# A four-layer convolution and attention kernel: another scheduling model, and a higher priority for the attention's work on VectorE and ScalarE

## The chip, the core and the metric

One core of a Trainium2 chip runs the whole kernel. The metric is the device time of one execution in microseconds (us); the figure that counts is the median of several runs. TensorE (PE in the profile; PEld is its loading of weights) multiplies matrices, VectorE (DVE) and ScalarE (ACT) work elementwise, GpSimd (POOL) does a few small powers, and SyncE (SP) issues all the DMAs. Every engine works through its own queue of instructions in order; semaphores tie the queues together.

## The reference

Four images of 256 channels and 64 x 64 points pass through four layers, each with a group normalisation before it and a residual sum behind it, all in float32.

```
x = x + L0(gn(x))   # 3x3 convolution, group norm, ReLU -> xs;  full attention over the
                    # 4096 points:  f = theta^T phi;  y = softmax(f) g;  1x1 conv, norm;  0.1*. + xs
x = x + L1(gn(x))   # linear attention: q, k, v of 4 heads x 32; context = k v^T; 1x1 conv, rms norms
x = x + L2(gn(x))   # generated kernels: depthwise 3x3 and pointwise 256x256, both from pooled x
x = x + L3(gn(x))   # mixture of four 256x256 experts, weights from pooled x
```

The attention of layer 0 has no shift by a row's maximum in the exponent here; sums are checked at the end and a general version would run if they left a safe range (it doesn't run with these inputs).

## The kernel before

The kernel is written in a tile language: the program text says what is computed in which tile, and a scheduler that plays the program through a model of the machine fixes the order of every engine's queue and the buffers. Among the instructions that are ready at a time of that model, the scheduler takes the one with the lowest priority number; the number counts up with the program text, so what stands earlier in the text goes first.

The work on an image falls into these parts.

- `convolve(b)`: group normalisation of the image in `xp`, a 3x3 convolution in a transformed (Winograd) form. `down` and `across` (DVE) make the inputs `v`, PE multiplies them with filters `u` that a DMA fetches from DRAM (`ps_conv`, line 325), DVE and ACT add the results up in `big`. Then a normalisation (`smoothed`), whose result xs stays in `big` and goes to DRAM (`xs_d`).
- `project()`: PE makes `theta`, `phi` and `g` from `big` (`ps_tp`, `ps_g`, lines 365 and 370) into the tile `tpg`.
- `attend(b)`: the full attention, in 8 query blocks of 512 points. A block has 16 steps `m`; a step makes two tiles `pf` = phi^T theta on PE (line 387), two exponentials on ACT into one tile `pr` (line 388), two products `py` += g pr on PE (line 397), and one sum `tot` += pr on DVE (recorded at the helper's line 62). The logits of step m+1 are written ahead of the products of step m. At the end of a block come `inv` (DVE, line 404), the column sum `pss` (PE, line 407), a reciprocal (DVE, line 408), a check value `junk` (ACT, line 410) and `yt` = py * inv (DVE), which a DMA writes to `y_d`.
- `tail(b)`: `nonlocal_out` (reads `y_d`, `ps_wy`, the residual of layer 0), `linear_attention` (layer 1), `generated` (layer 2: `dw`, eight multiply-adds a tile on DVE at the helper's line 65, then `ps_pw` on PE) and `mixed` (layer 3: `ps_ex`).

`pr` has three buffers, `pf` two banks of PSUM, `py` and `pss` share two banks, `tot` and `inv` have one buffer each. `junk` and `yt` share five buffers (`k2`) with small tiles of the layers.

`tpg` and `big` exist once. So `project()` for the next image waits until the attention on the present one is done and the next image's convolution too, and the next tail follows the projection. The loop over images is written so that the attention of image b, which comes last in the text of iteration b, stands beside the tail of image b-1 and the convolution of image b+1:

```
    for b in range(B):
        if b > 0:
            tail(b - 1)
        if b + 1 < B:
            load_x(b + 1)
            convolve(b + 1)
        attend(b)
        if b + 1 < B:
            project()
    tail(B - 1)
```

Of the kernel before, what the change touches and what calls it, by code (L numbers as in the profile page):

```python
# [8 lines left out]
F32 = mybir.dt.float32  # L9
AF = mybir.ActivationFunctionType  # L10
ALU = mybir.AluOpType
AX = mybir.AxisListType

P = 128
# [3 lines left out]
CH = 1024  # L18
# [21 lines left out]
def conv_preact_fast(ctx: ExitStack, tc: tile.TileContext, guard, x, wc, wtpg, ww, wqkv, wout, w1cat, wd2,  # L40
# [3 lines left out]
    nc = tc.nc  # L44
# [3 lines left out]
    wk = ctx.enter_context(tc.tile_pool(name="work", bufs=1))  # L48
    sp = ctx.enter_context(tc.tile_pool(name="small", bufs=2))
    pp = ctx.enter_context(tc.tile_pool(name="ps", bufs=1, space=bass.MemoryType.PSUM))  # L50
# [4 lines left out]
    def k2(name):  # L55
        return wk.tile([P, 512], F32, tag="k2", name=name, bufs=5)
# [4 lines left out]
    def tt(o, a, b, op):  # L61
        nc.vector.tensor_tensor(o, a, b, op)  # L62
# [18 lines left out]
    def load_x(b):  # L81
        for h in range(NH):
            for q in range(2):
                rows = bass.ts(q, HW // 2)
                nc.sync.dma_start(out=xin[:, h, rows, :],
                                  in_=x[b, bass.ts(h, P), bass.ts(q, N // 2)].rearrange("p (y x) -> p y x", x=HW))
# [32 lines left out]
    ones = cp.tile([P, P], F32, name="ones")  # L119
# [238 lines left out]
    def project():  # L358

        for c in range(N // 512):  # L360
            cols = bass.ts(c, 512)
            for k in (1, 0):
                ps = bank("ps_tp")
                for h in range(NH):
                    nc.tensor.matmul(ps, wtpg_s[:, h, k, :], big[:, h, cols], start=(h == 0), stop=(h == NH - 1))  # L365
                nc.scalar.activation(tpg[:, k, cols], ps, AF.Identity, bias=btp_s[:, k:k + 1])
            ps = bank("ps_g").rearrange("p (j o) -> p j o", o=P)
            for j in range(4):
                for h in range(NH):
                    nc.tensor.matmul(ps[:, j, :], big[:, h, bass.ts(4 * c + j, P)], wtpg_s[:, h, 2, :],  # L370
                                     start=(h == 0), stop=(h == NH - 1))
            tt(g[:, cols].rearrange("p (j o) -> p j o", o=P), ps, bg_s.unsqueeze(1).to_broadcast([P, 4, P]), ALU.add)

    def attend(b):
        NM = N // CH * 4
        for q in range(NQ):
            cols = bass.ts(q, 512)
            at = b * NQ + q
            py = pp.tile([P, 512], F32, tag="acc", name="py", bufs=2)
            tot = wk.tile([P, CH], F32, tag="tot", name="tot")  # L380
            probs = {}

            def logits(m):
                pr = wk.tile([P, CH], F32, tag="pr", name="pr", bufs=3)
                for s in range(2):
                    pf = pp.tile([P, 512], F32, tag="pf", name="pf", bufs=2)
                    nc.tensor.matmul(pf, phi[:, bass.ts(2 * m + s, P)], theta[:, cols], start=True, stop=True)  # L387
                    nc.scalar.activation(pr[:, bass.ts(s, 512)], pf, AF.Exp)  # L388
                probs[m] = pr

            logits(0)
            for m in range(NM):
                if m + 1 < NM:
                    logits(m + 1)
                pr = probs[m]
                for s in range(2):
                    nc.tensor.matmul(py, g[:, bass.ts(2 * m + s, P)], pr[:, bass.ts(s, 512)],  # L397
                                     start=(m == 0 and s == 0), stop=(m == NM - 1 and s == 1))
                if m == 1:
                    tt(tot, probs[0], pr, ALU.add)  # L400
                elif m > 1:
                    tt(tot, tot, pr, ALU.add)
            inv = wk.tile([P, 512], F32, tag="inv", name="inv")
            nc.vector.scalar_tensor_tensor(inv, tot[:, 0:512], 1.0, tot[:, 512:CH], ALU.mult, ALU.add,
                                           accum_out=guard[:, 0, at:at + 1])
            pss = pp.tile([P, 512], F32, tag="acc", name="pss", bufs=2)
            nc.tensor.matmul(pss, ones, inv, start=True, stop=True)  # L407
            nc.vector.reciprocal(inv, pss)  # L408
            junk = k2("junk")
            nc.scalar.activation(junk, inv, AF.Copy, accum_out=guard[:, 1, at:at + 1])  # L410
            yt = k2("yt")
            tt(yt, py, inv, ALU.mult)
            nc.sync.dma_start(out=y_d[b, :, cols], in_=yt)


# [237 lines left out]
    def tail(b):  # L653
        mixed(b, generated(b, linear_attention(b, nonlocal_out(b))))
# [3 lines left out]
    convolve(0)  # L658
    project()
    for b in range(B):  # L660
        if b > 0:
            tail(b - 1)
        if b + 1 < B:
            load_x(b + 1)
            convolve(b + 1)
        attend(b)
        if b + 1 < B:
            project()
    tail(B - 1)
# [502 lines left out]
@with_exitstack  # L1172
def conv_preact_kernel(ctx: ExitStack, tc: tile.TileContext, *args):
    nc = tc.nc
    B = args[0].shape[0]
    gp = ctx.enter_context(tc.tile_pool(name="guard", bufs=1))
    guard = gp.tile([P, 2, B * NQ + 1], F32, name="guard")
    conv_preact_fast(tc, guard, *args)


    fit = gp.tile([P, 2, B * NQ + 1], F32, name="fit")
    for side in range(2):
        nc.vector.tensor_scalar(fit[:, side, :], guard[:, side, :], GUARD_MAX[side], None, ALU.is_le)
    low = gp.tile([P, 1], F32, name="low")
    nc.vector.tensor_reduce(low, fit.rearrange("p s k -> p (s k)"), AX.X, ALU.min)
    every = gp.tile([P, P], F32, name="every")
    nc.gpsimd.memset(every, 1.0)
    good = gp.tile([P, 1], mybir.dt.int32, name="good")
    with tc.tile_pool(name="guard_ps", bufs=1, space=bass.MemoryType.PSUM) as gps:
        count = gps.tile([P, 1], F32, name="count")  # L1190
        nc.tensor.matmul(count, every, low, start=True, stop=True)
        nc.vector.tensor_scalar(good, count, P - 0.5, None, ALU.is_ge)
    in_range = nc.values_load(good[0:1, 0:1], min_val=0, max_val=1)
    with tc.If(in_range < 1):
        conv_preact_general(tc, *args)
# [58 lines left out]
```

## Time and profile before

| | |
|---|---|
| median of 3 runs | 3769.94 us (3769.51 to 3772.02) |
| the profiled execution | 3772.22 us |
| its span, first to last instruction | 3770.4 us |
| mean granted TensorE clock | 0.912 |
| busy: PE, DVE, ACT, POOL | 3150.8, 2208.6, 1125.4, 88.9 us |
| HBM traffic | 40 GB/s over the span |

The profile shows one execution. Its page gives busy times, then the span in 40 equal slices (a digit is a busy share in tenths), then groups of instructions with the mean duration of one. A view by stretches gives busy times between two moments. In this span the iterations of the loop lie, to a few us, at 225 to 802 (b = 0), 802 to 1709 (b = 1), 1709 to 2608 (b = 2) and 2608 to 3363 (b = 3); the tail of the last image follows to the end. Instructions of the small helpers for elementwise work on DVE are all recorded at lines 62 and 65, so that they are told apart by their tiles. Matmuls in float32 are recorded as two instructions each.

### The profile page before, as it was taken

Reading aid. Unit: us, or ns where it says so; the run is one execution under the profiler, and the core shown is the slowest. Engines: PE = TensorE matmul, PEld = TensorE weight load, DVE = VectorE, ACT = ScalarE, POOL = GpSimd, SP = SyncE. Lnnn points to the kernel's source line nnn. Section 1 sums busy time; section 2 is a strip of 40 time slices with the busy share of each in tenths; the row PEclk is TensorE's granted clock in tenths of the full one; section 3 lists DMA queues with packets and bytes.
Section 4 is the critical chain, followed back from the end, with each engine's and each line's share of the span. In section 5 each row is a group of like instructions: output and inputs, shape, how many; then the busy total and the mean of one; then the engine's idle time right before and its main releaser. Section 6 shows DMA issues by size and latency. Waiting matters only on the chain.

```text
span 3770.4 us, 24367 instructions
## 1 busy us (share of the span) xinstructions
PE 3150.8 (84%) x8322; PEld 1498.2 (40%) x8322; DVE 2208.6 (59%) x2696; ACT 1125.4 (30%) x2111; POOL 88.9 (2%) x133
## 2 busy tenths in 40 slices
PE   4699999989956889998984879999897699967645
PEld 2254444445422334444531334445452244434412
DVE  8869344353697944436479773444567734452476
ACT  2122333335410033333540013333443033323220
POOL 0000000001000000000100000000010000000000
PEclk9899999999977999999996889999998799987667
DMA  5313000020012220001001230000101200020011
GB/s 184 124 35 104 24 6 3 9 73 1 1 52 80 64 90 3 6 20 59 1 26 54 80 117 3 6 9 23 51 1 40 83 6 6 9 67 6 0 31 51
DMA packets 84484, 151.20 MB, mean 40 GB/s; under 512 B 8960, under 2 KB 46592, under 8 KB 82176
## 3 DMA queue, kind: packets, MB, share of 16 engines
q1 hardware_dynamic: 84352, 149.57, 11.6%
q8 instruction: 68, 1.11, 0.1%
q14 instruction: 64, 0.52, 0.0%
HBM read 101.30 MB, written 48.23 MB: 40 GB/s over the span
## 4 chain that ended last, share of the span: by engine, by line
PE 66%; DVE 21%; issue 7%; ACT 3%; POOL 2%; DMA 0%; SPq 0%; POOLq 0%; ACTq 0%; DVEq 0%
PE pf L387 20%; PE py L397 20%; PE ps_conv L325 9%; DVE dw L65 8%; PE ps_ex L647 3%; PE ps_tp L365 3%; DVE big L65 3%; PE ps_qkv L471 2%; PE ps_h L545 2%; PE ps_g L370 1%; PE ps_wy L425 1%; DVE z L62 1%; ACT junk L515 1%; DVE st L598 1%; PE ps_o L510 1%
## 5 line engine op out<-in xcount | busy, mean ns | idle before, releaser
L388 ACT ACTIVATE pr<-pf 128x512 f32<-128x512 f32 x1024 | 604.6, 596 | 1437.8 <-PE pf L387 1105.9
L62 DVE TENSOR_TENSOR tot<-tot,pr 128x1024 f32<-128x1024 f32 x448 | 547.9, 1223 | 826.1 <-ACT pr L388 825.7
L387 PE MATMUL pf<-tpg 128*128 128x512 f32 x2048 | 989.3, 605 | 22.7 <-ACT pr L388 22.7
L397 PE MATMUL py<-pr,tpg 128*128 128x512 f32 x2048 | 976.9, 600 | 11.1 <-DVE ev L62 7.7
L387 PEld LDWEIGHTS pf<-tpg 128*128 128x128 f32 x2048 | 385.7, 193 | 508.8 <-issue 419.1
L397 PEld LDWEIGHTS py<-pr,tpg 128*128 128x128 f32 x2048 | 390.6, 193 | 489.4 <-issue 471.7
L325 PE MATMUL ps_conv<-v,u 128*128 128x512 f32 x768 | 351.1, 618 | 88.3 <-issue 48.5
L595 PE MATMUL ps_pw<-dw,pk 128*128 128x512 f32 x256 | 158.8, 773 | 194.8 <-DVE dw L65 170.6
L65 DVE SCALAR_TENSOR_TENSOR dw<-xp,dk,dw 128x1008 f32<-128x1008 f32 (+1 forms) x256 | 309.9, 1262 | 6.4 <-ACT dw L582 6.2
L325 PEld LDWEIGHTS ps_conv<-v,u 128*128 128x128 f32 x768 | 151.2, 199 | 285.1 <-issue 239.4
L471 PE MATMUL ps_qkv<-wqkv_s,xg 128*128 128x384 f32 x512 | 190.3, 529 | 0.0
L595 PEld LDWEIGHTS ps_pw<-dw,pk 128*128 128x128 f32 x256 | 60.3, 250 | 292.0 <-DVE dw L65 187.4
L328 ACT COPY one<-ps_conv 128x512 f32<-128x512 f32 x48 | 28.1, 586 | 364.9 <-PE ps_conv L325 352.3
L408 DVE RECIPROCAL inv<-pss 128x512 f32<-128x512 f32 x32 | 107.4, 3356 | 42.9 <-PE pss L407 42.9
L471 PEld LDWEIGHTS ps_qkv<-wqkv_s,xg 128*128 128x128 f32 x512 | 103.6, 208 | 68.1 <-issue 16.0
L62 DVE TENSOR_TENSOR s<-sq 128x512 f32<-128x512 f32 x32 | 22.2, 692 | 182.5 <-ACT sq L455 182.5
L365 PE MATMUL ps_tp<-big,wtpg_s 128*128 128x512 f32 x256 | 118.9, 605 | 4.1 <-ACT big L304 4.1
L647 PE MATMUL ps_ex<-big,wm 128*128 128x512 f32 x256 | 119.2, 626 | 0.0
L202 PE MATMUL pm<-mv,avg 128*128 128x2 f32 x48 | 10.1, 279 | 127.8 <-DVE mv L198 96.6
L62 DVE TENSOR_TENSOR v<-ra 128x1024 f32<-128x1024 f32 x96 | 114.4, 1218 | 0.3
L62 DVE TENSOR_TENSOR tpg<-ps_g,bg_s 128x512 f32<-128x512 f32 x32 | 22.1, 690 | 118.1 <-PE ps_g L370 118.1
L138 POOL TENSOR_TENSOR rstd<-rstd,half 128x2 f32<-128x2 f32 x24 | 18.6, 773 | 3057.7 <-DVE rstd L212 3057.7
(176 smaller groups left out, 2679.3 us busy)
## 6 DMA issues: line engine op xcount, KB each, us to landing
u<-filters SPq DMA_DIRECT2D x192, 128.0 KB, 2.3
xp<-in_x_dram SPq DMA_DIRECT2D x16, 1024.0 KB, 5.1
xs_d<-big SPq DMA_DIRECT2D x32, 512.0 KB, 3.0
xs<-xs_d SPq DMA_DIRECT2D x32, 512.0 KB, 6.1
xr<-in_x_dram SPq DMA_DIRECT2D x32, 512.0 KB, 5.3
out_dram<-res SPq DMA_DIRECT2D x64, 256.0 KB, 2.0
y_d<-yt SPq DMA_DIRECT2D x32, 256.0 KB, 2.0
yt<-y_d SPq DMA_DIRECT2D x32, 256.0 KB, 2.9
```

The source lines that it names most:

```text
L62: nc.vector.tensor_tensor(o, a, b, op)
L65: nc.vector.scalar_tensor_tensor(o, a, s, b, op0, op1)
L325: nc.tensor.matmul(ps, u[:, h, :], vs[k][:, bass.ts(h, 512)], start=(h == 0), stop=(h == NH - 1))
L365: nc.tensor.matmul(ps, wtpg_s[:, h, k, :], big[:, h, cols], start=(h == 0), stop=(h == NH - 1))
L387: nc.tensor.matmul(pf, phi[:, bass.ts(2 * m + s, P)], theta[:, cols], start=True, stop=True)
L388: nc.scalar.activation(pr[:, bass.ts(s, 512)], pf, AF.Exp)
L397: nc.tensor.matmul(py, g[:, bass.ts(2 * m + s, P)], pr[:, bass.ts(s, 512)], start=(m == 0 and s == 0), stop=(m == NM - 1 and s == 1))
L408: nc.vector.reciprocal(inv, pss)
L471: nc.tensor.matmul(ps[:, 0:3 * HID], xg[:, h, bass.ts(j, P)], wqkv_s[:, h, :], start=(h == 0), stop=(h == NH - 1))
L545: nc.tensor.matmul(ps[0:2 * R, :], w1n[:, h, :], big[:, h, bass.ts(c, 512)], start=(h == 0), stop=(h == NH - 1))
L595: nc.tensor.matmul(ps, pk[:, h * NH * P + oh * P:h * NH * P + (oh + 1) * P], dw[h][:, bass.ts(s, 512)], start=(h == 0), stop=(h == NH - 1))
L647: nc.tensor.matmul(ps[oh], wm[:, h, bass.ts(oh, P)], big[:, h, cols], start=(h == 0), stop=(h == NH - 1))
```

## The change

Two things are done.

First, `attend` gets the priority number at the start of the iteration (`before`). The exponentials, the sums, and the whole closing part of a query block (`inv`, `pss`, the reciprocal, `junk`, `yt`) are written under `high_priority`, which sets their number back to `before`: to the number that the first instruction of the iteration's tail has. The matmuls `pf` and `py` and the DMA to `y_d` keep their late numbers.

Second, the call of the kernel's body stands in a block of its own, for which the scheduler uses another model of the machine, a simulation of its timeline, to decide what is ready when.

No instruction of the kernel's body is added, removed or given other operands.

```diff
-    def attend(b):
+    def attend(b, before):
+
+        def first():
+            return tc.high_priority(tc.cur_priority - before)
+
         NM = N // CH * 4
...
-                    nc.scalar.activation(pr[:, bass.ts(s, 512)], pf, AF.Exp)
+                    with first():
+                        nc.scalar.activation(pr[:, bass.ts(s, 512)], pf, AF.Exp)
                 probs[m] = pr
...
-                if m == 1:
-                    tt(tot, probs[0], pr, ALU.add)
-                elif m > 1:
-                    tt(tot, tot, pr, ALU.add)
...
+                with first():
+                    if m == 1:
+                        tt(tot, probs[0], pr, ALU.add)
+                    elif m > 1:
+                        tt(tot, tot, pr, ALU.add)
+            with first():
+                inv = wk.tile([P, 512], F32, tag="inv", name="inv")
+                nc.vector.scalar_tensor_tensor(inv, tot[:, 0:512], 1.0, tot[:, 512:CH], ALU.mult, ALU.add,
+                                               accum_out=guard[:, 0, at:at + 1])
+                pss = pp.tile([P, 512], F32, tag="acc", name="pss", bufs=2)
+                nc.tensor.matmul(pss, ones, inv, start=True, stop=True)
+                nc.vector.reciprocal(inv, pss)
+                junk = k2("junk")
+                nc.scalar.activation(junk, inv, AF.Copy, accum_out=guard[:, 1, at:at + 1])
+                yt = k2("yt")
+                tt(yt, py, inv, ALU.mult)
             nc.sync.dma_start(out=y_d[b, :, cols], in_=yt)
...
     for b in range(B):
+        before = tc.cur_priority
         if b > 0:
             tail(b - 1)
...
-        attend(b)
+        attend(b, before)
...
-    conv_preact_fast(tc, guard, *args)
+    with tc.block(name="fast", schedule_with_timeline_sim=True):
+        conv_preact_fast(tc, guard, *args)
```

More of the change, by code (lines that the diff above doesn't have):

```diff
@@ L398, in attend @@
                                      start=(m == 0 and s == 0), stop=(m == NM - 1 and s == 1))
-                if m == 1:
-                    tt(tot, probs[0], pr, ALU.add)
-                elif m > 1:
-                    tt(tot, tot, pr, ALU.add)
[L403 to L412, printed above, removed]
+                with first():
[14 more added lines that the diff above has]
+                tt(yt, py, inv, ALU.mult)
             nc.sync.dma_start(out=y_d[b, :, cols], in_=yt)
```

## The prediction

> **What bounds the kernel now.** I read the page's busy times first, then the busy times by stage, then the same stages for one tile, then the waits, and last a piece of the timeline. From the page:
>
> ```profile
> PE 3150.8 (84%) x8322; PEld 1498.2 (40%) x8322; DVE 2208.6 (59%) x2696; ACT 1125.4 (30%) x2111; POOL 88.9 (2%) x133
> PE   4699999989956889998984879999897699967645
> DVE  8869344353697944436479773444567734452476
> PEclk9899999999977999999996889999998799987667
> ```
>
> TensorE is busy for 84% of the span, and VectorE is busiest just where TensorE is not. The cause shows when the span is cut at the program's stages. Columns: stretch and its length, busy time of PE, PEld, DVE, ACT and POOL, granted clock, DMA share, GB/s.
>
> ```profile
> 265.00:802.00 537.00, 536.05 (x1340) 242.31 (x1339) 272.09 (x267) 175.32 (x294) 0.69 (x1) 1.00 0.09 31
> 802.00:865.00 63.00, 45.31 (x108) 20.33 (x107) 51.66 (x79) 21.07 (x35) 1.45 (x3) 0.84 0.27 88
> 865.00:1042.00 177.00, 170.16 (x629) 95.20 (x628) 89.66 (x141) 94.01 (x225) 18.09 (x24) 1.00 0.02 5
> 1042.00:1153.00 111.00, 56.32 (x99) 21.59 (x98) 108.75 (x120) 11.78 (x14) 0.00 (x0) 0.75 0.18 59
> 1153.00:1213.00 60.00, 38.62 (x98) 18.11 (x98) 36.91 (x63) 7.82 (x10) 2.30 (x2) 0.82 0.20 76
> 1213.00:1343.00 130.00, 100.04 (x209) 43.07 (x210) 117.25 (x141) 12.16 (x20) 0.70 (x1) 0.85 0.26 87
> 1343.00:1709.00 366.00, 366.00 (x946) 168.17 (x945) 141.06 (x119) 130.23 (x219) 0.00 (x0) 1.00 0.05 18
> 1709.00:2608.00 899.00, 767.01 (x2039) 360.11 (x2038) 544.17 (x659) 274.31 (x518) 22.55 (x30) 0.92 0.11 39
> 2608.00:3363.00 755.00, 663.22 (x1751) 311.49 (x1751) 415.41 (x498) 253.58 (x497) 20.24 (x28) 0.93 0.09 28
> 3363.00:3771.00 408.00, 230.55 (x631) 131.18 (x629) 224.09 (x327) 88.77 (x204) 19.33 (x28) 0.71 0.09 31
> ```
>
> The rows from 802 to 1709 are iteration b=1: tail of image 0 (802 to about 1197), convolution of image 2 (to 1343), then attention alone and the projection. The next two rows are iterations 2 and 3, the first is iteration 0, the last is the tail of image 3. Iteration 1 takes 907 us, in which PE works 776 and stands for 131; DVE works 545. From 1042 to 1343 DVE is full and PE starves; from 1343 on PE is full and DVE has 39%. The same stages for `tot`, the attention's running sum on DVE:
>
> ```profile
> 865.00:1042.00 177.00, 26.07 (x23) 1.00 0.02 5
> 1042.00:1153.00 111.00, 0.00 (x0) 0.75 0.18 59
> 1153.00:1213.00 60.00, 3.66 (x3) 0.82 0.20 76
> 1213.00:1343.00 130.00, 3.13 (x4) 0.85 0.26 87
> 1343.00:1709.00 366.00, 112.02 (x100) 1.00 0.05 18
> ```
>
> The x counts are the sums and what reads them, 17 a query block and 136 an image. In 301 us DVE does 7 of them. So attention does not lack PE there; it lacks a turn on DVE. The waits of ACT between 802 and 1343 (total, times, longest) close the loop:
>
> ```profile
> ACT pr L388 <- DVE tot L62: 93.2, 1, 93.2
> ```
>
> The timeline shows PE's side:
>
> ```profile
> 1065.74 1.45 PE L387 MATMUL pf<-tpg 128*128 128x512 f32 x3
> 1065.80 14.27 DVE L65 SCALAR_TENSOR_TENSOR dw<-xp,dk,dw 128x1008 f32<-128x1008 f32 x12
> 1077.76 2.07 PE L595 MATMUL ps_pw<-dw,pk 128*128 128x512 f32 x2 [10.57 <-DVE dw L65]
> ```
>
> An exponential waits 93.2 us for a sum, since `pr` has three buffers; with no exponential `pf` stays full, and PE stands 10.6 us for the depthwise product.
>
> **Part 1: exponentials, sums and the closing of a query block move ahead on ACT and DVE.** Nothing is added or removed; the order changes.
>
> What a query block costs. From 1400 to 1600, attention alone, PE runs 230 `pf`, 230 `py` and 6 `pss` instructions in 200 us: 0.429 us each. A block has 64 + 64 + 2 = 130, so 55.8 us of PE, 446 for an image. On DVE it has 15 sums of 1.22, the 0.69 of `inv`, 3.36 of the reciprocal and 0.69 of `yt`: 23.1 us. On ACT 32 exponentials of 0.596 and the check's 0.82: 19.9.
>
> What else PE must do in iteration 1. 512-column instructions: 192 `ps_conv`, 64 each of `ps_pw`, `ps_ex`, `ps_tp`, 32 each of `ps_wy`, `ps_h`: 448 x 0.429 = 192 us. Narrower ones by their columns (an estimate): 128 `ps_qkv` 41, 64 `ps_o` 14, 288 of 128 columns 31, the rest 11. Together 289, so PE's need is 446 + 289 = 735 us at full clock, against 907. Iteration 3 has no convolution and projection (82 + 27 + 14): 612 against 755.
>
> Whether DVE and the layers' chain allow it, stage by stage; T is the stage's new length, n the blocks done in it.
> - 1042 to 1153: DVE's own work is 108.75 and PE's is 64 x 0.429 = 27.5. Both full: 108.75 + 23.1n = 27.5 + 55.8n, n = 2.5, T = 166. The layers lose 55 us here, PE gains 138 us of attention.
> - 1153 to 1343: DVE's own 146, PE's own 256 x 0.429 = 110. Both full gives n = 1.1 and T = 171, less than the present 190, so the chain of small steps sets T; I take 200, n = 1.6.
> - 802 to 865: PE's own 13.7; T = 68, n = 0.9. 865 to 1042: PE full already, T = 177, n = 167/128 = 1.3.
> - Sum: T = 611, n = 6.3; the other 1.7 blocks take 95 and the projection 41: 747. Iteration 3 in the same way (68 + 177 + 166 + 60, n = 5.2, then 2.8 blocks): 627.
>
> Where attention and layers share PE now, it is busy 96% (865 to 1042) and 99.8% (iteration 0, with a convolution). No row shows both engines saturated, so I allow for 94 to 96%: 790 for iterations 1 and 2, 655 for iteration 3. Gain: (907 - 790) + (899 - 790) + (755 - 655) = 326 us. The cover is DVE's idle 59% from 1343 on; what is late next is the layers' chain, behind at most one sum (1.22 us) or reciprocal (3.36 us) at a time.
>
> The clock: the stages' rows show it at 0.75 to 0.85 where PE has gaps, 1.00 where it has none. If it stayed at iteration 1's 0.92, 735 would be 795, about what I took.
> By the Trainium skill's page "TensorE: Matmul & The Clock Gate" (Part 1: The HAM clock gate), half speed comes only after an idle window of about 3.4 us, so short gaps would keep 735 to 747 and the gain would be some 440 us (estimate); no row shows so dense a mix for long outside iteration 0.
>
> A rule speaks against the change: "Perfetto Trace Analysis" (Optimization Strategy) puts repeated gaps on the engine that should be full down to missing SBUF or PSUM for the next tile, and this change adds no buffer to `pr`; by that alone the time stays at 3770. The 93.2 us row says otherwise: the buffer is held by a sum that was queued late.
>
> Moves with one answer: `pss` goes first on PE too (2 instructions a block, 27 us in all, unchanged); `junk` and `yt` take their `k2` buffers earlier, five of them serve all; the `y_d` write keeps its place behind the convolution's filter loads on SP, where it is needed only by the next tail. Prologue (265 us), iteration 0 (PE 99.8% busy) and the last tail (408 us, no attention to mix in): nothing.
>
> **Part 2: the order comes from the timeline's model, inside a block of its own.** Nothing in the trace prices it. The nearest rows: PE's waits for `ps_conv` on "issue" (three, 16.2 us in iteration 1), which a better order of filter loads could remove, so some -45 us over the kernel; the other way, a PE order that puts a layer's matmul before its input is ready costs what `ps_pw` waits now, 46.6 us an iteration, +140. I take 0, as iteration 0 shows an order that holds on the chip. The block's two edges: 0 to 10 us.
>
> **Sum.** The profiled execution took 3772.2 us for a span of 3770.4; less 326 it is 3446, and as the median (3769.94) lies 2 under it, 3444.
>
> **The rivals.**
> 1. *The mix is only half as dense.* Queues run in order, and an order worked out ahead meets other durations here: PE stands at a layer's matmul while attention's is ready behind it. For it: the 46.6 us at `ps_pw`. Against: 96% and 99.8%. If half of the gain stays away, 3772 - 163 = 3609 (3570 to 3700).
> 2. *Slower: sums at DVE's head wait for their exponentials and hold the layers.* DVE now waits 17.2 us for `pr` over the 37 steps on `tot` between 802 and 1343, 0.5 each. Suppose six more blocks' DVE and ACT work lies wholly on the layers' chain: 541 + 6 x 43 = 799, and 41 for the projection, 840. That is still 67 under 907, so it decides from 67/96 = 0.7 us of waiting for each of the 96 moved sums, beyond their own time. At 1.5 us (two `pf` instructions and an exponential: 0.86 + 0.6) it is 984, +77 in each of two iterations and some +40 in the third: about 3960; at 1.0 us about 3850. Against: the order of all queues comes from one schedule, and PE has its operands ready in iteration 0's mix.
> 3. *Nothing moves.* PE's order is not moved ahead except `pss`, so if PE's queue set the pace, 3760 to 3780. Against: 0.00 for `tot` while PE stands.
>
> **How the numbers follow.** Forecast 0.60 (its own range 3380 to 3540), rival 1 0.21, rival 2 0.13, rival 3 0.06. Rival 3 lies half within 0.2% (about what a measurement of this kernel can tell from no change) and half just outside. Faster 0.83, same 0.03, slower 0.14. The range 3350 to 3700 reaches from the clock's and the filter loads' gain to the end of rival 1 and leaves out rivals 2 and 3 and little more.
>
> **What would show it.** Right: `tot` runs throughout each iteration, some 35 to 45 steps on it during the depthwise stage; PE is at 93% or more from 265 to about 3040; the clock there is 0.97 or more; iterations 1 and 2 last 750 to 830 us, the depthwise stage grows past 150; the stretch of attention alone shrinks from 330 to under 120 us. Wrong: DVE's waits for `pr` inside the layers' stages exceed 60 us an iteration, or PE stands at the end of an iteration for the convolution with attention used up.

## The result, and the profile after

The changed kernel takes 3964.95 us (median; 3961.73 to 3965.13) against 3770.86 for the kernel before on the same chip: a ratio of 1.0513, 95% interval 1.0495 to 1.0531. The forecast was 3444. The profiled execution took 3961.73 us for a span of 3959.9, at a mean granted clock of 0.894 (0.912 before). The page, with the lines that answer to those shown of before:

```profile
PE 3183.0 (80%) x8322; PEld 1532.9 (39%) x8322; DVE 2213.1 (56%) x2696; ACT 1134.1 (29%) x2111; POOL 86.7 (2%) x133
PE   4699999999626899998952689999895389995627
DVE  8769434372477954336248793443624944445466
PEclk9899999999767999999966799999997689997768
```

The work is the same, but TensorE is filled less: each iteration now has a deeper hole: 626, 526 and 53 in PE's row, where before it had 56, 848 and 76. Cut at the stages of iteration 1, from the last image's tail to the projection (columns as before):

```profile
804.00:907.00 103.00, 93.37 (x207) 40.57 (x207) 71.83 (x95) 35.49 (x61) 1.45 (x3) 0.92 0.18 61
907.00:1013.00 106.00, 103.13 (x381) 60.87 (x379) 30.11 (x49) 56.84 (x117) 8.45 (x15) 0.98 0.00 1
1013.00:1116.00 103.00, 59.00 (x174) 37.12 (x175) 46.42 (x78) 29.52 (x89) 8.75 (x9) 0.69 0.02 5
1116.00:1231.00 115.00, 40.65 (x68) 16.04 (x66) 108.40 (x120) 9.31 (x10) 0.00 (x0) 0.64 0.17 58
1231.00:1292.00 61.00, 34.40 (x88) 16.97 (x88) 35.46 (x63) 4.44 (x4) 1.39 (x2) 0.78 0.21 78
1292.00:1400.00 108.00, 90.01 (x194) 37.89 (x194) 106.47 (x119) 7.66 (x14) 0.00 (x0) 0.91 0.27 86
1400.00:1779.00 379.00, 378.87 (x973) 174.03 (x974) 148.59 (x143) 136.82 (x228) 0.70 (x1) 0.99 0.05 20
```

The rows are: `ps_wy` and what follows to the linear attention; `ps_ss` to `ps_ctx`; `ps_o`, `ps_zt` and `ps_h` (the z stage); depthwise and `ps_pw`; experts; convolution; attention and projection. The same view for the tile `pf` (PE, PEld, ACT), with the last four layers' stages as one:

```profile
804.00:907.00 103.00, 43.34 (x78) 14.99 (x77) 23.43 (x40) 0.92 0.18 61
907.00:1013.00 106.00, 27.10 (x54) 9.72 (x54) 14.69 (x25) 0.98 0.00 1
1013.00:1400.00 387.00, 0.00 (x0) 0.00 (x0) 0.00 (x0) 0.75 0.16 55
```

In 387 us not one logit is computed, while PE stands for 163 of them. The kernel before had 87 `pf` instructions (46.33 us) between 945 and 1335. The products `py` of two query blocks of image 1 start at 805 and 890, those of the third at 1400; before, two started at 820 and 967 and the third at 1335. So both kernels get two blocks, and no more, beside the layers; the changed one uses them up early. What holds the third, from three pieces of the timeline:

```profile
886.57 3.36 DVE L415 RECIPROCAL inv<-pss 128x512 f32<-128x512 f32 x1 [0.55 <-PE pss L414]
...
1386.42 0.59 ACT L328 COPY one<-ps_conv 128x512 f32<-128x512 f32 x1 [7.55 <-PE ps_conv L325]
1386.90 0.63 ACT L417 ACTIVATE junk<-inv 128x512 f32<-128x512 f32 x1
1387.02 0.68 DVE L62 TENSOR_TENSOR yt<-py,inv 128x512 f32<-128x512 f32 x1
...
1396.78 3.29 DVE L415 RECIPROCAL inv<-pss 128x512 f32<-128x512 f32 x1
1400.13 0.50 PEld L402 LDWEIGHTS py<-pr,tpg 128*128 128x128 f32 x2 [6.12 <-DVE inv L415]
```

The first block's reciprocal ends at 889.9. Its `junk` and `yt` need nothing else but a `k2` buffer, and run 497 us later, right behind the convolution's last `one`, which is a `k2` tile too. Until then `py` of block 0 keeps one `acc` bank, `py` of block 1 the other, `pss` of block 1 has none, and `inv` and `tot` (one buffer each) are held. In the kernel before the same reciprocal ended at 967.1 and its `yt` started at 1327.88:

```profile
963.79 3.35 DVE L408 RECIPROCAL inv<-pss 128x512 f32<-128x512 f32 x1
...
1327.88 0.63 DVE L62 TENSOR_TENSOR yt<-py,inv 128x512 f32<-128x512 f32 x1
```

That a `k2` buffer is what these two instructions lack is, up to here, a reading; the experiments test it.

### The profile page after: what moved, and what is told of

It is laid out like the page before. It is cut to its first block, busy times and chain, and to the rows that moved or that the text cites. A ratio compares the mean times of both kernels' runs of the same rounds, so it can differ in the third digit from the quotient of the medians.

```text
span 3959.9 us, 24425 instructions
## 1 busy us (share of the span) xinstructions
PE 3183.0 (80%) x8322; PEld 1532.9 (39%) x8322; DVE 2213.1 (56%) x2696; ACT 1134.1 (29%) x2111; POOL 86.7 (2%) x133
## 5 line engine op out<-in xcount | busy, mean ns | idle before, releaser
L62 DVE TENSOR_TENSOR tot<-tot,pr 128x1024 f32<-128x1024 f32 x448 | 547.9, 1223 | 948.1 <-ACT pr L393 947.7
L391 PE MATMUL pf<-tpg 128*128 128x512 f32 x2048 | 1040.3, 599 | 20.3 <-ACT pr L393 20.3
L402 PE MATMUL py<-pr,tpg 128*128 128x512 f32 x2048 | 1035.5, 601 | 25.6 <-DVE inv L415 13.6
L602 PE MATMUL ps_pw<-dw,pk 128*128 128x512 f32 x256 | 147.8, 739 | 284.1 <-DVE pk L65 234.8
L529 PE MATMUL ps_zt<-ident,z 128*128 128x128 f32 x256 | 62.2, 425 | 144.8 <-DVE z L62 144.8
L522 ACT ACTIVATE junk<-z 128x256 f32<-128x256 f32 x128 | 52.0, 407 | 228.2 <-DVE z L62 228.2
L62 DVE TENSOR_TENSOR v<-ra 128x1024 f32<-128x1024 f32 x96 | 112.5, 1217 | 2.8 <-PE ps_conv L325 2.7
L529 PEld LDWEIGHTS ps_zt<-ident,z 128*128 128x128 f32 x256 | 50.2, 224 | 162.0 <-issue 142.7
L517 PE MATMUL ps_o<-w,xp 128*128 128x256 f32 x256 | 102.7, 573 | 1.9 <-ACT w L508 1.9
```

What stands on the lines that cost most here:

```text
L517: nc.tensor.matmul(ps[:, j, :], qT[:, bass.ts(4 * c + 2 * s + j, P)], w2, start=True, stop=True)
L529: nc.tensor.transpose(pt[:, bass.ts(j, P)], z[:, j, bass.ts(h, P)], ident)
L602: nc.tensor.matmul(ps, pk[:, h * NH * P + oh * P:h * NH * P + (oh + 1) * P], dw[h][:, bass.ts(s, 512)], start=(h == 0), stop=(h == NH - 1))
```

## The experiments

Three theories for why no gain came and 194 us were lost. **A, buffers:** a tag's buffers go to its tiles in the order of the text, whatever their priority, and the closing of `attend(b)` stands behind all `k2` tiles of tail and convolution. **B, waits:** rival 2, sums at DVE's head hold the layers. **C, the model:** the timeline's order of the layers' own work is slower; in the course of it **E, place**: the model's order puts the two blocks where they cost most. In the table "own closing" means that the closing uses no `k2` buffer; "chain" is the time of the layers in iteration 1, from the first `ps_wy` to the last `ps_conv`; ratios are against the kernel before run beside it (3771.6 to 3772.4).

| run | us | ratio (95%) | chain |
|---|---|---|---|
| before (profiled) | 3772.2 | | 517 |
| after (profiled) | 3961.7 | | 581 |
| part 1 alone | 3770.61 | 0.9996 (0.9986 to 1.0005) | 530 |
| part 2 alone | 3963.28 | 1.0508 (1.0490 to 1.0525) | 581 |
| before, own closing | 3639.08 | 0.9649 (0.9633 to 0.9665) | 526 |
| both parts, own closing | 3487.34 | 0.9248 (0.9233 to 0.9263) | 734 |
| part 1, own closing | 3350.02 | 0.8882 (0.8867 to 0.8897) | 613 |
| part 2, own closing | 3492.86 | 0.9259 (0.9244 to 0.9275) | 737 |
| after, six `k2` buffers | 3966.75 | 1.0518 (1.0497 to 1.0539) | 580 |
| part 2, blocks late | 3867.72 | 1.0246 (1.0229 to 1.0263) | 556 |
| before, blocks late | 3829.65 | 1.0153 (1.0136 to 1.0170) | 531 |
| before, no block beside | 4118.44 | 1.0919 (1.0901 to 1.0937) | 535 |
| part 2, no block beside | 4086.19 | 1.0837 (1.0819 to 1.0855) | 518 |
| own closing, sums ahead only | 3553.28 | 0.9420 (0.9404 to 0.9436) | 557 |

A shorter chain isn't better by itself: with seven blocks beside it 613 us are well spent.

**The two parts, each alone.** The kernel after without the block of part 2:

```diff
-    with tc.block(name="fast", schedule_with_timeline_sim=True):
-        conv_preact_fast(tc, guard, *args)
+    conv_preact_fast(tc, guard, *args)
```

> Only part 1: the priorities of the exponentials, sums and closings, without the block that takes the order from the timeline's model. Theory A (buffers): in both kernels exactly two query blocks of an image close beside the layers, because `junk` and `yt` get their `k2` buffers only after all small tiles of the tail and the convolution, which stand earlier in the text. Then priority alone can't start a third block before the convolution ends; it only moves the two forward, so the time lies between the two kernels, 3780 to 3960. Theory B (waits): sums put ahead on DVE wait for exponentials and hold the layers; then this part alone carries the whole loss, about 3965. Theory C (model): the loss is the model's order of the layers' own work; then this part alone gives 3770 or less.

3770.61: no change within the interval, and the blocks of image 1 start at 813, 885 and 1327, just behind the convolution (1325). All 120 sums of an iteration (15 a block) are moved ahead as in the changed kernel, and it costs nothing. B falls, for the loss seen here. A holds in that no third block comes, but expected some loss. C stands. The closing of the first block, with its early priority, still runs only behind the convolution's last `one` (1318.98):

```profile
1319.81 0.67 DVE L62 TENSOR_TENSOR yt<-py,inv 128x512 f32<-128x512 f32 x1
```

The kernel before with the block of part 2 put around the same call:

> Only part 2: the block with the timeline's model, without the priorities. A: still two query blocks, and on PE's queue they stand in the same places as in the kernel after (one before and one behind the 16 ps_wy, nothing of attention until the 96 ps_conv are done), so about 3965, within 10. B: without the priorities no sum is put ahead, so 3770 to 3800. C: the model's order is there, 3965.

3963.28, with starts at 805, 890 and 1400 as in the kernel after: part 2 carries the whole loss, as A and C expected.

**The closing without `k2` buffers.** The same two lines in the kernels after and before:

```diff
-                junk = k2("junk")
+                junk = tot[:, 0:512]
...
-                yt = k2("yt")
+                yt = inv
```

> The kernel after, with the check value `junk` written into the first half of `tot` and `yt` written over `inv`, so that a query block's closing takes no `k2` buffer; same instructions, same number of buffers. A: the third block starts some 60 to 120 us after the second instead of 510 us after it, the blocks spread over the whole iteration (iteration 1 at 750 to 850 us instead of 975), 3450 to 3600. B: more sums are ahead of the layers than before, so no gain: 3965 or more. C: the layers' order stays the model's, so 3900 to 3965.

> The kernel before with the same change of destinations (`junk` into `tot`, `yt` into `inv`). A: the third block may now close beside the layers, but its steps still have late priorities and get a turn on DVE only where the layers leave one, so about one block more per iteration: 3600 to 3740. B and C: nothing that they name is touched, 3760 to 3780.

3487.34 and 3639.08, both in A's range. With both parts the blocks of image 1 start at 811, 882, 974, 1059, 1130, 1264, 1341 and 1459, and `ps_wy` to `ps_wy` takes 803 us instead of 975. With neither, three blocks start beside the layers (821, 968, 1171). Same instructions, same number of buffers: what changed is that the closing's two tiles need no `k2` buffer.

**Which part works once the blocks can close.** The two lines with part 1 alone and with part 2 alone:

> Part 1 alone (priorities, no timeline's model) on top of the closing without `k2` buffers (`junk` in `tot`, `yt` in `inv`). If priority is what brings the blocks forward once a third can start, this is as good as the full change with the same closing (3487): 3450 to 3530. If the model's order is what spreads them, it stays near the 3639 that the kernel before gives with this closing.

> Part 2 alone (the timeline's model, no priorities) with the closing without `k2` buffers. PE's queue is then nearly the one of the full change with this closing (each of the blocks 2 to 7 within a few layers' matmuls of its place there). If the model sets the order and priority adds nothing to it: 3470 to 3510. If priority is needed for the gain: 3560 to 3640.

Part 1 alone gives 3350.02, better than expected, and the fastest kernel here: 420 us under the kernel before. Part 2 alone gives 3492.86, and both parts 3487.34, with overlapping intervals: under the model the priorities make no difference that these runs can tell. Against the default order the model is worth 146 us where the attention's work is late (3639 to 3493) and costs 137 us where it is ahead (3350 to 3487): it mixes the two by itself, but less well than the priorities do. The page and five stages of iteration 1 of the fastest kernel (`ps_wy`; `ps_ss` to `ps_ctx`; z stage; depthwise; experts):

```profile
PE 3061.4 (91%) x8322; PEld 1464.1 (44%) x8322; DVE 2190.4 (65%) x2696; ACT 1121.5 (33%) x2111; POOL 91.8 (3%) x133
PE   3789999999999999999999999999999999948545
PEclk9899999999999999999999999999999999967667
```

```profile
796.00:868.00 72.00, 70.93 (x175) 31.28 (x173) 62.05 (x88) 30.72 (x51) 1.45 (x3) 1.00 0.24 77
868.00:950.00 82.00, 81.54 (x335) 50.58 (x335) 28.52 (x48) 49.63 (x108) 10.26 (x15) 1.00 0.01 4
950.00:1060.00 110.00, 103.84 (x329) 51.01 (x327) 69.79 (x100) 50.17 (x129) 9.12 (x9) 1.00 0.02 6
1060.00:1214.00 154.00, 153.78 (x357) 66.50 (x357) 149.44 (x153) 52.46 (x87) 0.00 (x0) 1.00 0.13 43
1214.00:1287.00 73.00, 72.38 (x184) 32.06 (x182) 53.03 (x83) 18.22 (x29) 1.83 (x2) 1.00 0.21 79
```

The depthwise stage shows what the change was for: PE 153.78 and DVE 149.44 of 154 us, at the full clock.

With both parts and the own closing, PE's waits from 265 to 2940 (total, times, longest) show a part of what the model loses: the exponentials come late, and PE waits 63.8 us for them, 20 times and up to 4.8 us. With part 1 alone the same row has 0.8 us. The rest of the 137 us isn't traced to one cause.

```profile
PE pf L391 <- ACT pr L393: 63.8, 20, 4.8
```

**Order, or number, of buffers.** The kernel after with one more `k2` buffer, and room for it:

```diff
-        return wk.tile([P, 512], F32, tag="k2", name=name, bufs=5)
+        return wk.tile([P, 512], F32, tag="k2", name=name, bufs=6)
...
-                    u = wk.tile([P, NH, P], F32, tag="u", name="u", bufs=4)
+                    u = wk.tile([P, NH, P], F32, tag="u", name="u", bufs=3)
```

> The kernel after with six `k2` buffers instead of five (and three `u` buffers instead of four, for room); `junk` and `yt` still in `k2`. Theory A says that what holds the third block is the order in which a tag's buffers are handed out (by the text), not their number: the third block of image 1 still starts within 15 us of 1400, 3940 to 3990. The rival, that five buffers are simply too few at the time: the third block starts 60 us or more earlier and the time falls below 3900.

3966.75, third block at 1401. One more buffer changes nothing, and `yt` again follows the last `one` (1387.86 behind 1387.24). With the runs below, in which two other tags follow the text as well, this speaks for the order and not the count; a larger number of buffers wasn't tried.

**Where the 193 us of part 2 come from.** First the two blocks moved behind the linear attention's context, with A's own rule as the gate: tiles that stand earlier in the text take the `acc` buffers first.

```diff
-        pctx = bank("ps_ctx")
+        pctx = pp.tile([P, 512], F32, tag="acc", name="ps_ctx", bufs=2)
...
-        pt = bank("ps_cm")
+        pt = pp.tile([P, 512], F32, tag="acc", name="ps_cm", bufs=2)
...
-        pw = bank("ps_w2")
+        pw = pp.tile([P, 512], F32, tag="acc", name="ps_w2", bufs=2)
```

> Part 2 alone, closing as in the kernel before (two blocks beside the layers), but `ps_ctx`, `ps_cm` and `ps_w2` of the linear attention take buffers of the tag `acc` that `py` and `pss` use; they stand earlier in the text, so the first query block starts only behind them, on PE's queue beside `ps_o` and `ps_zt`. Why is the model's order 195 us slower with the same two blocks? Theory E (place): it spends both blocks beside ps_wy to ps_ctx, where PE is full without help, and leaves the z stage, where PE waits for the layers, empty; then this kernel gets most of the loss back: 3730 to 3850, ps_wy to ps_ctx some 150 us instead of 209. Theory C (the model's order of the layers' own work): no change or worse, 3950 to 4050.

3867.72: half of the loss comes back, 18 us above E's range. `ps_wy` to `ps_ctx` takes 145 us (806 to 951) instead of 202, near E's 150, but the z stage grows, from 104 us to 134 (951 to 1085), now that the blocks sit there with PE full (131.10 us of the 132 to 1083). The default order with the same gate:

> The kernel before with `ps_ctx`, `ps_cm` and `ps_w2` in the tag `acc`, so that its two query blocks also start behind the linear attention's context. Against the run with the model and the same late start (3868) this has the default order. E: place decides, so both end alike, 3770 to 3870, with the blocks now beside the z, depthwise and expert stages. C: the default order stays about 190 us ahead: 3650 to 3700.

3829.65, in E's range, and only 38 us from the run with the model. With the blocks in the same place the difference of 193 us is down to 38, and that remainder stays unexplained. Last, no block at all beside the layers:

```diff
-                pr = wk.tile([P, CH], F32, tag="pr", name="pr", bufs=3)
+                pr = k4("pr")
```

> The kernel before with `pr` taken from the tag `k4` (seven buffers, shared with the layers' tiles) instead of its own three: by theory A no query block then starts before the convolution of the next image has its last `k4` tile, so all eight run alone, in iteration 0 too. It gives the length of the layers' chain without attention beside it. Estimate from the stages in which the kernel after has no attention (103 z and h, 115 depthwise, 61 experts, 108 convolution) and some 150 for ps_wy to ps_ctx: chain about 540, iteration 1 about 540 + 8 x 56 + 40 = 1030, the whole 4150 to 4300. If A is wrong on the order of buffers, attention runs beside the layers as before: 3770.

> The same with part 2 (the timeline's model, no priorities). Theory E (the loss of part 2 is where it puts the two query blocks): with no block beside the layers the two orders cost the same, within 40 us of the run without the model. Theory C (the model's order of the layers' own work is slower): the difference of 193 us between part 2 alone and the kernel before remains, 150 to 220 us slower than the run without the model. As the late start of the two blocks gave back half of it, a half may remain: 60 to 120.

4118.44 and 4086.19. In both the first block's products start behind the last `ps_conv` (at 1366 and 1350 in iteration 1), so a third tag follows the order of the text (4118 lies 32 us under the range of the estimate). Without blocks the model's order is 32 us faster than the default order, not 193 slower: C falls. So the loss arises where blocks and layers meet. In the default order two blocks are worth 4118 - 3770 = 348 us over the kernel, in the model's order 4086 - 3963 = 123. The column "chain" says the same: 518 with the model and no block, 581 with two; in the default order 535 and 517.

**Which of part 1's moves matters.** Only the sums on `tot` ahead, own closing:

```diff
-                    with first():
-                        nc.scalar.activation(pr[:, bass.ts(s, 512)], pf, AF.Exp)
+                    nc.scalar.activation(pr[:, bass.ts(s, 512)], pf, AF.Exp)
...
-            with first():
-                inv = wk.tile([P, 512], F32, tag="inv", name="inv")
+            inv = wk.tile([P, 512], F32, tag="inv", name="inv")
```

The closing's other lines stand outside `first()` in the same way.

> Of part 1 only the sums on `tot` moved ahead (not the exponentials, not the closing), closing without `k2` buffers, default model. With all of part 1 it is 3350, with none 3639. If the sums are what attention lacks a turn for, as the prediction read it: nearer to 3350, 3350 to 3460. On PE's queue four blocks instead of seven start before the convolution's end (three with none of part 1), so the closing's place may matter as much: then 3500 to 3600.

3553.28: 86 of the 289 us between 3639 and 3350. Image 1's fifth block starts only at 1371, behind the convolution (1359). The sums alone are not what attention lacked: the other 203 us come when the exponentials and the closing move too. Which of these two brings how much, no run shows.

## Why the prediction was wrong

Two steps failed: one took the gain away, the other made the loss.

**The step that took the gain away** is the clause "`junk` and `yt` take their `k2` buffers earlier, five of them serve all". They did not take them earlier; a higher priority doesn't pass a tile that stands before it in the text and wants the same tag. All blocks beyond the second in the stages' n rested on that. Its effect alone: where the forecast has a gain of 326 us, part 1 brought 0 (3770.61). With the two lines that free the closing the gain is 420, of which these lines alone bring 131 (3639.08) and the priorities on top of them 289.

**The rest of part 1's sum was right, for the kernel without that hold.** Forecast against the run with part 1 and own closing (`tot` instructions by 17 a block):

| | T, n forecast | T, n measured |
|---|---|---|
| `ps_wy` | 68, 0.9 | 72, 0.9 |
| `ps_ss` to z | 177, 1.3 | 192, 1.6 |
| depthwise | 166, 2.5 | 154, 2.2 |
| experts, convolution | 200, 1.6 | 195, 1.5 |
| all four | 611, 6.3 | 613, 6.3 |

The iterations last 755, 755 and 629 us (`ps_wy` to `ps_wy`) against sums of 747 and 627 and the 790 and 655 that were taken; the allowance for 94 to 96% was too much, as PE ran at 99% (746.47 of 755), at a clock of 1.00 in every stage. The prediction's other estimate, a gain of some 440 us for a clock that stays full, was the nearer one. That the four stages agree to 2 us in all is partly luck: they miss by -12 to +15 us one by one. Three slips in the prediction's readings change little: DVE is idle for 61% from 1343 on (141.06 of 366 us busy), not 59; from 1042 to 1343 it is busy for 87% (262.9 of 301), not full; and 735 us at a clock of 0.92 are 799, not 795.

**The step that made the loss** is part 2's "I take 0". Beside the priorities it cost 194 us with two blocks (3770.61 to 3964.95) and 137 with the own closing, against bounds of -45 to +140. The row taken as evidence, iteration 0, couldn't show it: it has the default model's order, and no tail that attention could get in the way of. The price came where none of the prediction's rows looked: the model's order sets both blocks beside `ps_wy` to `ps_ctx`, and these take 202 us instead of 143.

**The row `ACT pr L388 <- DVE tot L62: 93.2, 1, 93.2`** was read as a sum that lacks a turn. That is half of it: the second block's last three sums did wait for a turn, until 1157.7, and with blocks free to close, priority is worth 289 us. But with the closing blocked, the turn was worth nothing: from 1162 on the second block's sums are done, and no third block starts before 1335. What the prediction didn't read is the end of a block: between the first block's reciprocal (ready at 967.1) and its `yt` (1327.88) lay 361 us in which none of its operands was missing.

**The rule that was weighed and dismissed pointed the right way.** The Trainium skill's "Perfetto Trace Analysis" (Optimization Strategy) says that a repeated gap on the engine that should be full can mean too little SBUF or PSUM for the next tile. The prediction concluded from it that "by that alone the time stays at 3770", and part 1 alone stayed at 3770.61. It looked for the missing buffer at `pr` and not at the block's last two tiles. The page names the number of buffers and the size of tiles, though; here one more buffer changed nothing (3966.75), while taking the two tiles out of the `k2` order did.

**The rivals.** Rival 2's price, 3960, met the time by accident: its mechanism is refuted by the two parts run each alone (3770.61 with the sums ahead, 3963.28 without), and by the 3350.02 with all blocks free to run. In the changed kernel DVE waits 38.0 us for `pr` between 804 and 1400, 16 times; with both parts and own closing 84.2 us over the chain, in a kernel that is 478 us faster. So the sign "DVE's waits for `pr` exceed 60 us" was badly chosen. Rival 3 is what part 1 alone did, for a reason the prediction didn't have: not PE's queue but `k2`.

**What stays open.** Why the timeline's model sets the blocks' matmuls among `ps_wy` to `ps_ctx`, where PE has no room, and lets exponentials come late, isn't shown by any run; only that it does, and that the layers' chain pays 63 us an iteration for it (581 against 518).

## What to carry to other kernels

Before work is moved ahead, follow one unit of it to its last instruction and ask which buffers it must give back: if one of them has a tag that earlier text uses too, priority doesn't help, and giving the closing tile a place of its own (or writing it over an operand that is dead) may be worth more than the move: here 131 us alone, against nothing for the move alone. Change a scheduler's model and its priorities one at a time: here the priorities alone were worth nothing and the model cost 193 us, but once a two-line hold is gone the priorities are worth 289 us. A wait whose releaser has a late place in the queue has two readings, a lack of turn and a lack of room, and only the last instruction of the unit tells them apart.

## What the runs showed of the hardware

The same work of the layers ran at three clocks. The stage `ps_ss` to `ps_ctx` without attention beside it in the default order, the same in the model's order, and with attention in the kernel before:

```profile
885.00:985.00 100.00, 85.46 (x284) 56.48 (x284) 18.34 (x39) 42.39 (x92) 8.43 (x15) 0.76 0.00 0
```

```profile
890.00:972.00 82.00, 71.47 (x282) 47.10 (x282) 18.08 (x38) 42.12 (x92) 8.45 (x15) 0.90 0.00 1
```

```profile
865.00:945.00 80.00, 79.76 (x331) 50.06 (x331) 25.43 (x44) 48.30 (x104) 9.35 (x15) 1.00 0.00 1
```

A `ps_qkv` instruction takes 650, 557 and 491 ns in them. With 47 instructions more the third is 20 us shorter than the first, but only 2 us shorter than the second: load is one way to the full clock, another order of the same instructions goes most of the way. In the first, PE's gaps sum up to 14.5 us and the longest that lies within the stretch is 2.9 us (one of 4.7 us ends 0.7 us after its start); yet the clock lies between 0.67 and 0.81 in each 20 us of it. Cut finer it is 0.50 or 1.00: 0.50 from 899.2 to 905.9, with PE busy all the time, and 1.00 from 906.0 to 912.7, with PE busy for 4.92 of 6.70 us. The Trainium skill's "TensorE: Matmul & The Clock Gate" (Part 1: The HAM clock gate), which the prediction cited, has half speed come after an idle window of about 3.4 us, but tells also of a kernel in which PE's frequent short idles made the clock swing between half and full speed; the first stretch is of that second kind. Short gaps alone don't decide: in the z stage of the fastest kernel (950 to 1060 above) PE has gaps of 6.2 us, none over 1.2, and the clock is 1.00. How much idle time is too much, no run here shows. Work that fills PE's gaps can thus be worth more than its own time, as in the default order here, as long as the layers don't queue behind it.
